# Two-layer convolution kernel: the second channel block convolved by ScalarE and VectorE, statistics on ScalarE, v with two slots

## The chip, the cores and the metric

The kernel runs on one core of a Trainium2 chip. The metric is device time in microseconds, the median of the runs. The core has TensorE (PE) for matrix products, VectorE (DVE), ScalarE (ACT) and GpSimd (POOL) for elementwise work, and SyncE (SP), which issues nearly all DMA transfers. Each engine executes its own instructions in order; semaphores tie the engines together.

## The reference

The input is `x` of shape (16, 56, 56, 384) in fp32. Two layers follow each other:

```
x = x + attention(group_norm(x))     # layer 0
x = x + depthwise(group_norm(x))     # layer 1
```

`group_norm` takes 32 groups of 12 channels, with mean and variance over all 56 x 56 positions of an image. `attention` projects to q, k and v (384 channels each), splits them into three blocks of 128 channels with dilations 1, 2 and 3 and four heads of 32 channels each, and for every position scores q against the nine k at the 3 x 3 neighbours (dilated, zero padded), takes the softmax of the nine, sums the nine v with these weights, and projects back. `depthwise` is a 3 x 3 convolution per channel whose weights are the signs of the given ones, zero padded.

## The kernel before, in words

Channels lie on the partitions in three blocks `j` of 128. An image is cut into seven chunks of eight rows (448 positions), which makes 112 chunks `m`; a chunk is the unit of everything. Three plans give the pieces of work of a chunk. `plan_a` loads `x` and turns it so that channels lie on the partitions (`turn`, L409), takes statistics and writes it to `xd` in device memory. `plan_b` is layer 0: it normalises a chunk of `xd`, projects k and v (`k_or_v`, L467) and q, multiplies q with the shifted k on VectorE (`score`, L508), sums over the head by PE, takes the softmax, spreads the weights over the channels by PE into the PSUM tile `pb_a` (a pool with one buffer), multiplies them with the shifted v on VectorE (`weigh`, L573, L589), adds on GpSimd (L597 to L601), projects back (`out_project`, L607), takes statistics (L621) and writes `x1d`. `plan_c` is layer 1 for one chunk.

The time of a piece is a slice number; a chunk advances by `STEP = 9` slices. Pieces are emitted in the order of (slice, kind), and the framework's scheduler then settles each engine's order, with these as priorities. Layer 1 of a chunk runs ten chunks behind layer 0 of it, since it needs the statistics of the whole image. So in the steady part all three plans run side by side. For the last image, layer 1 runs after everything else.

Layer 1 before the change: channel blocks 0 and 1 (`JG = 2`) are loaded three times with a row's shift as `z` (L694), normalised by four ScalarE instructions (L713), and convolved by PE (`convolve`, L721, twelve products in four column groups, result `pc`), and VectorE adds `x1` (L734). Block 2 is loaded once as `xg`, normalised into the padded tile `zg` (L756), multiplied by nine taps on ScalarE (`taps_g`, L778) and summed on GpSimd (L784 to L792). For the last image block 2 is instead accumulated by VectorE (`taps_last`, L769). Then PE turns the chunk back (`turn`, L794) and ScalarE evacuates it to `osb`, which goes out.

Transposes, projections and convolutions share the PSUM pool `ps_mt` of three buffers. k has two slots per dilation, v has three; each chunk's tile takes border rows from the one before and gives it some, by DMA on SP's queue (L477, L478). Pieces that matter below:

```python
at(t0 - 12 + 3 * g, QKV, lambda g=g: k_or_v(g, 0))
at(t0 - 9 + 3 * g, QKV, lambda g=g: k_or_v(g, 1))
at(t0 + 14 + i, WEIGH, lambda i=i: weigh(i))
at(t0 + 2 + 3 * j + late, CONVOLVE, lambda j=j: convolve(j))
at(t0 + 9 + s, STAGE_C, lambda s=s: turn(s))
```

Of the kernel before, what the change touches and what calls it, by code (L numbers as in the profile page):

```python
# [12 lines left out]
ALU = mybir.AluOpType  # L13
# [15 lines left out]
NPAD = 32  # L29
K_SLOTS, V_SLOTS = 2, 3  # L30
RSQRT_BITS = 0x5F3759DF
# [4 lines left out]
def dilated_attention_then_binary_conv(  # L36
# [36 lines left out]
    K3 = 3 * HD  # L73
    JG = NG - 1

# [61 lines left out]

    ktap = const.tile([P, NTAP], F32, name="ktap")

    kdiag = const.tile([K3, 3, JG * NQ, HD], F32, name="kdiag")  # L140

    xin_p = ctx.enter_context(tc.tile_pool(name="xin_p", bufs=1))
    z_p = ctx.enter_context(tc.tile_pool(name="z_p", bufs=2))
    xa_p = ctx.enter_context(tc.tile_pool(name="xa_p", bufs=3))
    st_p = ctx.enter_context(tc.tile_pool(name="st_p", bufs=2))
# [8 lines left out]
    x1_p = ctx.enter_context(tc.tile_pool(name="x1_p", bufs=2))  # L154
    xg_p = ctx.enter_context(tc.tile_pool(name="xg_p", bufs=2))
    m_p = ctx.enter_context(tc.tile_pool(name="m_p", bufs=2))
    o_p = ctx.enter_context(tc.tile_pool(name="o_p", bufs=2))

# [16 lines left out]


    zg = []
    for s in range(2):
        t = const.tile([P, ROWS + 2, W + 2], F32, name=f"zg_{s}")
        nc.gpsimd.memset(t, 0.0)  # L180
        zg.append(t)
# [12 lines left out]
    def load_small_weights():  # L194

        raw["small"] = t = m_p.tile([P, 3, PX], F32, tag="m", name="small")
        flat = t.rearrange("p k n -> p (k n)")
        at_ = [0]

        def room(parts, n):  # L200
            at_[0] += n
            return flat[:parts, at_[0] - n : at_[0]]

        raw["b"] = room(NG, P)
        raw["k"], raw["kp"] = room(K3, 3 * NG * NQ), room(K3, 3 * NG * NQ)
        raw["kg"] = room(P, NTAP)
        raw["eye"] = room(K3, HD)
        raw["spread"] = room(P, 2 * P)
        raw["clipped"], raw["less"] = room(P, 3 * NG * NQ), room(P, 3 * NG * NQ)
        nc.sync.dma_start(raw["b"], b_proj.rearrange("(j p) -> j p", p=P))  # L210
        nc.sync.dma_start(raw["kg"], w_conv.rearrange("y x c m -> c (y x m)")[JG * P : (JG + 1) * P, :])

# [19 lines left out]
    def small_weights():  # L232
# [29 lines left out]
        kp = raw["kp"].rearrange("p (k s) -> p k s", k=3)  # L262
        binary(ktap, raw["kg"])
        eye3 = raw["eye"]
# [30 lines left out]
    def group_norm(stats, done, for_convolution=False):  # L295
# [79 lines left out]
        return channels, mean, deviation, variance, invert, spread_out  # L375

    def chunk_of(dram, c):
        return dram.rearrange("(j p) n -> p j n", p=P)[:, :, c * PX : (c + 1) * PX]
# [12 lines left out]
    def plan_a(m, t0):  # L391
# [4 lines left out]
        def load():  # L396
            if c == 0:
                stats0[b] = st_p.tile([P, NG, NCH, 6], F32, tag="stats0", name="stats0")
                xd[b] = dr_p.tile([C, H * W], F32, tag="xd", name="xd")
            if b == 0 and c % 3:  # L400

                xin = z_p.tile([P, NQ * PX], F32, tag="z", name="xin_z")[:SUB, : NSUB * C]
                xin = xin.rearrange("p (s c) -> p s c", s=NSUB)
            else:
                xin = xin_p.tile([SUB, NSUB, C], F32, tag="xin", name="xin")
# [3 lines left out]
        def turn(j):  # L409
# [12 lines left out]
            else:  # L422
                xa = xa_p.tile([P, PX], F32, tag="xa", name="xa")
            nc.scalar.copy(xa, pt[:, :PX])  # L424
            nc.vector.bn_stats(stats0[b][:, j, c, :], xa)
            if b:
# [18 lines left out]
    def plan_b(m, t0):  # L445
# [84 lines left out]
        def softmax_1():  # L530

            sT = s_p.tile([P, PX], F32, tag="sT", name="sT")
            nc.scalar.copy(sT, had.pop("ps")[:, :PX])
# [21 lines left out]
        def softmax_3():  # L555

            had["rest"] = rest = s_p.tile([SUB, NSUB * NPAD * HEADS], F32, tag="rest", name="rest")
            nc.scalar.copy(term[0], e8)
# [48 lines left out]
        def out_project(j):  # L607

            if c == 0 and j == 0:
                stats1[b] = st_p.tile([P, NG, NCH, 6], F32, tag="stats1", name="stats1")  # L610
                x1d[b] = dr_p.tile([C, H * W], F32, tag="x1d", name="x1d")
            xr = had["xr"]
            po = ps_mt.tile([P, 512], F32, tag="mt", name="po")
            for g in range(NG):
                nc.tensor.matmul(  # L615
                    po[:, :PX], wprojT[:, g, j * P : (j + 1) * P], had[f"y{g}"], start=(g == 0), stop=(g == NG - 1)
                )
            nc.vector.scalar_tensor_tensor(  # L618
                xr[:, j, :], po[:, :PX], bias[:, j : j + 1], xr[:, j, :], op0=ALU.add, op1=ALU.add
            )  # L620
            nc.vector.bn_stats(stats1[b][:, j, c, :], xr[:, j, :])  # L621
            if j == NG - 1:
# [12 lines left out]
        for g in range(NG):  # L635
            at(t0 - 12 + 3 * g, QKV, lambda g=g: k_or_v(g, 0))
            at(t0 - 9 + 3 * g, QKV, lambda g=g: k_or_v(g, 1))
            at(t0 - 1 + 3 * g, QUERY, lambda g=g: query(g))
# [16 lines left out]
    def plan_c(m, t0):  # L655
# [17 lines left out]
        def load(j):  # L673
# [4 lines left out]
            else:  # L678

                had[f"z{j}"] = []  # L680
                for q0 in range(0, NQ, 2):
                    pool, tag = (t_p, "t") if c % 2 == 0 else (w_p, "w") if (j, q0) != (1, 2) else (xr_p, "xr")
                    z = pool.tile([P, 3, PX], F32, tag=tag, name="z_last")[:K3, :2]
# [33 lines left out]
        def load_x():  # L717
            had["x1"] = x1 = x1_p.tile([P, JG, PX], F32, tag="x1", name="x1")
            nc.sync.dma_start(x1, chunk_of(x1d[b], c)[:, :JG])  # L719

# [18 lines left out]
        def load_g():  # L739
            if b < B - 1:  # L740
                had["xg"] = xg = xg_p.tile([P, ROWS + 2, W], F32, tag="xg", name="xg")
            else:
# [3 lines left out]
                xg[:, lo:hi, :].rearrange("p r w -> p (r w)"),  # L746
                x1d[b][JG * P : (JG + 1) * P, p0 + (lo - 1) * W : p0 + (hi - 1) * W],
            )

        def normalise_g():  # L750
            if c == 0:
                nc.gpsimd.memset(zp[:, 0], 0.0)
            if c == NCH - 1:
# [3 lines left out]
                zp[:, lo:hi, 1 : W + 1], had["xg"][:, lo:hi, :], AF.Identity,  # L757
                bias=mr[:, JG, 0:1], scale=mr[:, JG, 1:2],
            )

        def taps_last(ky):
# [5 lines left out]
            for kx in range(3):  # L767
                o = 3 * ky + kx
                nc.vector.scalar_tensor_tensor(  # L769
                    mid if o == 8 else acc, zp[:, ky : ky + ROWS, kx : kx + W], ktap[:, o : o + 1],  # L770
                    acc if o else mid, op0=ALU.mult, op1=ALU.add,
                )

        def taps_g(ky):
            t = m_p.tile([P, 3, PX], F32, tag="m", name="m")
            for kx in range(3):
                o = 3 * ky + kx
                nc.scalar.activation(  # L778
                    rows(t[:, kx]), zp[:, ky : ky + ROWS, kx : kx + W], AF.Copy, scale=ktap[:, o : o + 1]
                )  # L780
# [13 lines left out]
        def turn(s):  # L794
            pt = ps_mt.tile([P, 512], F32, tag="mt", name="pt_o")
            mid = had["xg"][:, 1 : ROWS + 1, :].rearrange("p r w -> p (r w)")
            for j in range(NG):
                src = mid if j == JG else had["x1"][:, j]
                nc.tensor.transpose(pt[:SUB, j * P : (j + 1) * P], src[:, s * SUB : (s + 1) * SUB], ident)  # L799
            osb = o_p.tile([SUB, C], F32, tag="osb", name="osb")  # L800
            nc.scalar.copy(osb, pt[:SUB, :C])  # L801
# [4 lines left out]
        if b == B - 1:  # L806
# [9 lines left out]
            for ky in range(3):  # L816
                at(t0 + 1 + ky, CONVOLVE, lambda ky=ky: taps_last(ky))
            for s in range(NSUB):
                at(t0 + 12, STAGE_C, lambda s=s: turn(s))
# [10 lines left out]
        for j in range(JG):  # L830
            at(t0 - 4 + 3 * j, LOADS, lambda j=j: load(j))
            at(t0 - 1 + 3 * j + late, NORM, lambda j=j: normalise(j))
            at(t0 + 2 + 3 * j + late, CONVOLVE, lambda j=j: convolve(j))
        for s in range(NSUB):
            at(t0 + 9 + s, STAGE_C, lambda s=s: turn(s))

# [50 lines left out]
```

## Time and profile before

| | |
|---|---|
| median of 3 runs | 5416.96 us (5413.93 to 5419.03) |
| the profiled execution | 5406.89 us |
| its span | 5405.2 us |
| mean granted TensorE clock | 0.98 |
| busy: PE, DVE, ACT, POOL | 5205.9, 4150.0, 2397.8, 4215.2 us |
| DMA | 825.73 MB, mean 153 GB/s |

The profile is of one execution. A row of its groups names the line, the engine, the operation, what it writes and reads with its shape, how often, then busy time, mean duration of one in ns, and the engine's idle time ahead of it with what ended that. A line of waits names who waited for whom, the microseconds in total, the number of waits and the longest. PE's end times are modelled, so a length from start to start says more than the duration printed.

### The profile page before, as it was taken

What the parts mean: (1) busy time and instruction counts of PE and PEld (TensorE: products, weight loads), DVE (VectorE), ACT (ScalarE), POOL (GpSimd) and SP (SyncE); (2) the same over time, 40 slices, a digit from 0 to 9 for tenths busy, and PEclk for the clock granted to TensorE, in tenths of its full rate; (3) what the DMA queues carried; (4) which work ended last, traced back from release to release, by engine and by line L of the source; (5) the groups of instructions that cost most, each with busy time, mean ns of one, the idle gap of its engine ahead of it and who ended that gap; (6) DMA issues with size and microseconds to landing.
All of it is one profiled execution on the core that took longest, in us unless ns stands there. A gap on an engine that the chain in (4) does not pass through costs nothing. (4 is left out here: it accounts for less than half of the span.)

```text
span 5405.2 us, 77297 instructions
## 1 busy us (share of the span) xinstructions
PE 5205.9 (96%) x27669; PEld 2414.4 (45%) x27669; DVE 4150.0 (77%) x4209; ACT 2397.8 (44%) x4189; POOL 4215.2 (78%) x3049
## 2 busy tenths in 40 slices
PE   8999999999999999999999999999999999999965
PEld 4444444444444444444444444444444444444422
DVE  4887777878777787777777777787777778777754
ACT  3224444444444444444444444444444444444433
POOL 2677888888888887888888788888888888888880
PEclk9999999999999999999999999999999999999976
DMA  5444555655555555555655655555555655544443
GB/s 168 127 120 124 159 157 158 163 154 161 158 158 160 164 159 159 157 157 158 163 154 161 164 152 160 164 157 163 159 157 154 164 154 161 161 130 134 122 130 126
DMA packets 810799, 825.73 MB, mean 153 GB/s; under 512 B 359467, under 2 KB 800174, under 8 KB 810414
## 3 DMA queue, kind: packets, MB, share of 16 engines
q1 hardware_dynamic: 802430, 808.79, 54.2%
q10 hardware_dynamic: 7984, 12.00, 0.7%
q8 instruction: 219, 3.59, 0.3%
q14 instruction: 166, 1.36, 0.1%
HBM read 466.41 MB, written 231.21 MB: 129 GB/s over the span
## 5 line engine op out<-in xcount | busy, mean ns | idle before, releaser
L597 POOL TENSOR_TENSOR w<-w 128x1344 f32<-128x1344 f32 x672 | 2049.9, 3050 | 456.2 <-DVE w L589 396.7
L589 DVE TENSOR_TENSOR w<-pb_a,v 128x1344 f32<-128x1344 f32 x1008 | 1559.1, 1547 | 267.0 <-PE pb_a L582 177.4
L516 DVE TENSOR_TENSOR t<-pq,k 128x1344 f32<-128x1344 f32 x1008 | 1535.8, 1549 | 237.0 <-PE pq L463 236.1
L463 PE MATMUL pkv<-xn,wqkvT 128*128 128x448 f32 x3924 | 1569.9, 549 | 9.0 <-ACT xa L424 4.7
L463 PEld LDWEIGHTS pkv<-xn,wqkvT 128*128 128x128 f32 x3924 | 718.4, 190 | 671.8 <-issue 629.4
L615 PE MATMUL po<-y,wprojT 128*128 128x448 f32 x2016 | 834.9, 550 | 27.4 <-POOL y L601 15.0
L784 POOL TENSOR_TENSOR m<-m 128x1344 f32<-128x1344 f32 x210 | 644.7, 3070 | 274.1 <-ACT m L778 274.0
L463 PE MATMUL pq<-xn,wqkvT 128*128 128x448 f32 x1962 | 830.7, 558 | 0.0
L713 ACT ACTIVATE z<-z,mrz 96x448 f32<-96x448 f32 x840 | 578.3, 751 | 350.9 <-DMA z<-x1d 330.3
L501 PE MATMUL ps<-t,sel 128*32 128x448 f32 x6048 | 666.0, 550 | 26.0 <-DVE t L516 25.3
L778 ACT ACTIVATE m<-zg,ktap 128x448 f32<-128x448 f32 x945 | 555.5, 658 | 274.0 <-POOL m L784 266.9
L615 PEld LDWEIGHTS po<-y,wprojT 128*128 128x128 f32 x2016 | 376.4, 191 | 382.9 <-issue 341.1
L727 PE MATMUL pc<-z,kdiag 96*32 96x440 f32 (+1 forms) x5040 | 516.7, 543 | 6.4 <-POOL z L715 4.6
L463 PEld LDWEIGHTS pq<-xn,wqkvT 128*128 128x128 f32 x1962 | 344.0, 189 | 316.9 <-issue 316.9
L734 DVE TENSOR_TENSOR x<-pc,x 128x448 f32<-128x448 f32 x224 | 139.3, 622 | 353.2 <-PE pc L727 342.1
L582 PE MATMUL pb_a<-aT,spread 24*128 24x448 bf16 x3024 | 369.1, 359 | 32.2 <-DVE w L589 25.9
L601 POOL TENSOR_TENSOR y<-y,w 128x448 f32<-128x448 f32 x336 | 381.5, 1135 | 22.6
L618 DVE SCALAR_TENSOR_TENSOR xr<-po,bias,xr 128x448 f32<-128x448 f32 x336 | 227.5, 677 | 220.9 <-PE po L615 217.2
L600 POOL TENSOR_TENSOR y<-w 128x448 f32<-128x448 f32 x336 | 382.2, 1138 | 14.7
L473 ACT COPY v<-pkv 128x448 f32<-128x448 f32 x336 | 178.3, 531 | 484.1 <-PE pkv L463 475.8
L473 ACT COPY k<-pkv 128x448 f32<-128x448 f32 x336 | 178.2, 530 | 376.5 <-PE pkv L463 376.5
L501 PEld LDWEIGHTS ps<-t,sel 128*32 128x32 f32 x6048 | 170.6, 110 | 364.9 <-issue 247.8
(131 smaller groups left out, 4394.7 us busy)
## 6 DMA issues: line engine op xcount, KB each, us to landing
z<-x1d SPq DMA_DIRECT2D x570, 224.0 KB
xr<-xd SPq DMA_DIRECT2D x112, 672.0 KB
x1d<-xr SPq DMA_DIRECT2D x112, 672.0 KB
xn<-xd SPq DMA_DIRECT2D x109, 672.0 KB
xin<-in_x_dram SPq DMA_DIRECT2D x108, 672.0 KB
xd<-xa SPq DMA_DIRECT2D x315, 224.0 KB
out_dram<-osb SPq DMA_DIRECT2D x420, 168.0 KB
x<-x1d SPq DMA_DIRECT2D x112, 448.0 KB
```

The lines of the kernel that those rows point to most:

```text
L463: nc.tensor.matmul(dst[:, :PX], wqkvT[:, cc, o0 : o0 + P], had["xn"][:, cc, :], start=(cc == 0), stop=(cc == NG - 1))
L501: return nc.tensor.matmul(had["ps"][32 * j : 32 * j + 32, :PX], sel[:, s0 : s0 + 32], tk, start=(issued[j] == 1), stop=(issued[j] == len(r ...
L516: nc.vector.tensor_tensor(t.rearrange("p k (r w) -> p k r w", w=W), q3, k3, ALU.mult)
L589: nc.vector.tensor_tensor(w.rearrange("p k (r w) -> p k r w", w=W), pb[:, :, :PX].rearrange("p k (r w) -> p k r w", w=W), three(kv[1][g][m ...
L597: nc.gpsimd.tensor_tensor(w0, w0, w, ALU.add)
L600: nc.gpsimd.tensor_tensor(y, w0[:, 0], w0[:, 1], ALU.add)
L601: nc.gpsimd.tensor_tensor(y, y, w0[:, 2], ALU.add)
L615: nc.tensor.matmul(po[:, :PX], wprojT[:, g, j * P : (j + 1) * P], had[f"y{g}"], start=(g == 0), stop=(g == NG - 1))
L713: nc.scalar.activation(z, z, AF.Identity, bias=mrz[:, j, q, 0:1], scale=mrz[:, j, q, 1:2])
L727: return nc.tensor.matmul(pcr[q * HD : (q + 1) * HD, :, lo:hi], kdiag[:, kx, j * NQ + q, :], rows(set_of(j, q))[:, :, lo + kx - 1 : hi + k ...
L778: nc.scalar.activation(rows(t[:, kx]), zp[:, ky : ky + ROWS, kx : kx + W], AF.Copy, scale=ktap[:, o : o + 1])
L784: nc.gpsimd.tensor_tensor(had["m"], had["m"], t, ALU.add)
```

## The change

Layer 1 keeps PE for block 0 alone (`JG = 1`). Block 2 (`JS = 2`) stays as it was. Block 1 is convolved in a new way: `load_b` loads it once as `xb`, `normalise_b` normalises it into a third padded tile, `taps_b` multiplies it by the nine taps on ScalarE into nine slices of the tile `m9`, `load_summand` loads the block itself into a tenth slice, and `sum_b` sums the ten on VectorE in four parts of 112 positions. `m9` and `xb` have one buffer each. The `BATCH_NORM_STATS2` instructions on VectorE go: the sum of a tile comes from an accumulator output of the instruction that writes it, ScalarE scales it to the mean and sums the squared deviations by a second accumulator output (`statistics`). v of a chunk is computed nine slices later and has two slots. Pools shrink to make room (`z_p` 2 to 1, `xa_p` 3 to 2), and `rest` shares its buffer with `sT`. The diff, without the declarations of pools and the loading of the small weights, which follow from it:

```diff
-K_SLOTS, V_SLOTS = 2, 3
+K_SLOTS, V_SLOTS = 2, 2
-    JG = NG - 1
+    JG = 1
+    JS = NG - 1
+    NB = NG - JG
...
-    z_p = ctx.enter_context(tc.tile_pool(name="z_p", bufs=2))
-    xa_p = ctx.enter_context(tc.tile_pool(name="xa_p", bufs=3))
+    z_p = ctx.enter_context(tc.tile_pool(name="z_p", bufs=1))
+    xa_p = ctx.enter_context(tc.tile_pool(name="xa_p", bufs=2))
...
+    m9_p = ctx.enter_context(tc.tile_pool(name="m9_p", bufs=1))
+    xb_p = ctx.enter_context(tc.tile_pool(name="xb_p", bufs=1))
...
+    def new_statistics(name):
+        stats = st_p.tile([P, NG, NCH, 3], F32, tag=name, name=name)
+        nc.gpsimd.memset(stats[:, :, :, 0:1], float(PX))
+        return stats
+
+    def statistics(entry, xa, total):
+        nc.scalar.mul(entry[:, 1:2], total, 1.0 / PX)
+        squares = st_p.tile([P, PX], BF16, tag="squares", name="squares", bufs=1)
+        nc.scalar.activation(
+            squares, xa, AF.Square, bias=entry[:, 1:2], scale=-1.0, accum_out=entry[:, 2:3]
+        )
...
-            if b == 0 and c % 3:
+            if b == 0 and c % 2:
...
-            nc.scalar.copy(xa, pt[:, :PX])
-            nc.vector.bn_stats(stats0[b][:, j, c, :], xa)
+            total = st_p.tile([P, 1], F32, tag="total", name="total")
+            nc.scalar.activation(xa, pt[:, :PX], AF.Copy, accum_out=total)
+            statistics(stats0[b][:, j, c, :], xa, total)
...
             nc.vector.scalar_tensor_tensor(
-                xr[:, j, :], po[:, :PX], bias[:, j : j + 1], xr[:, j, :], op0=ALU.add, op1=ALU.add
-            )
-            nc.vector.bn_stats(stats1[b][:, j, c, :], xr[:, j, :])
+                xr[:, j, :], po[:, :PX], bias[:, j : j + 1], xr[:, j, :], op0=ALU.add, op1=ALU.add, accum_out=total
+            )
+            statistics(stats1[b][:, j, c, :], xr[:, j, :], total)
...
-            at(t0 - 9 + 3 * g, QKV, lambda g=g: k_or_v(g, 1))
+            at(t0 + 3 * g, QKV, lambda g=g: k_or_v(g, 1))
...
-            nc.sync.dma_start(x1, chunk_of(x1d[b], c)[:, :JG])
+            nc.sync.dma_start(x1[:, :JG], chunk_of(x1d[b], c)[:, :JG])
...
+        def load_b():
+            had["xb"] = xb = xb_p.tile([P, ROWS + 2, W], F32, tag="xb", name="xb")
+            nc.sync.dma_start(
+                xb[:, lo:hi, :].rearrange("p r w -> p (r w)"),
+                x1d[b][JG * P : (JG + 1) * P, p0 + (lo - 1) * W : p0 + (hi - 1) * W],
+            )
+
+        zb = zg[2]
+
+        def normalise_b():
...
+            nc.scalar.activation(
+                zb[:, lo:hi, 1 : W + 1], had["xb"][:, lo:hi, :], AF.Identity,
+                bias=mr[:, JG, 0:1], scale=mr[:, JG, 1:2],
+            )
+
+        def load_summand():
+            had["m9"] = m9 = m9_p.tile([P, NTAP + 1, PX], F32, tag="m9", name="m9")
+            nc.sync.dma_start(m9[:, NTAP], x1d[b][JG * P : (JG + 1) * P, p0 : p0 + PX])
+
+        def taps_b(o):
+            ky, kx = divmod(o, 3)
+            nc.scalar.activation(
+                rows(had["m9"][:, o]), zb[:, ky : ky + ROWS, kx : kx + W], AF.Copy, scale=ktap[:, 0, o : o + 1]
+            )
+
+        def sum_b(s):
+            part = slice(s * SUB, (s + 1) * SUB)
+            nc.vector.reduce_sum(
+                had["x1"][:, JG, part], had["m9"][:, :, part].rearrange("p o n -> p n o"), axis=AX.X
+            )
...
+            at(t0 - 4, LOADS, load_b)
+            at(t0 + 2, NORM, normalise_b)
+            at(t0 + 2, LOADS, load_summand)
+            for o in range(NTAP):
+                at(t0 + 3 + o // 3, CONVOLVE, lambda o=o: taps_b(o))
+            for s in range(NSUB):
+                at(t0 + 7 + s, CONVOLVE, lambda s=s: sum_b(s))
...
+        at(t0 - 1, LOADS, load_b)
+        at(t0 + 1, NORM, normalise_b)
+        at(t0 + 1, LOADS, load_summand)
+        for o in range(NTAP):
+            at(t0 + 2 + (0, 1, 1, 1, 2, 3, 3, 3, 4)[o], CONVOLVE, lambda o=o: taps_b(o))
         for s in range(NSUB):
+            at(t0 + 7 + s, CONVOLVE, lambda s=s: sum_b(s))
             at(t0 + 9 + s, STAGE_C, lambda s=s: turn(s))
```

The first group of times in the last two blocks is that of the last image.

## The prediction

> **What bounds the kernel now.** I read the page's busy shares, then whole-image stretches of the steady part, then who keeps TensorE (PE) waiting, one stretch in order of time, and the rows of the operations concerned. The page first:
>
> ```profile
> PE 5205.9 (96%) x27669; PEld 2414.4 (45%) x27669; DVE 4150.0 (77%) x4209; ACT 2397.8 (44%) x4189; POOL 4215.2 (78%) x3049
> ```
>
> A stretch of seven chunks, one image (columns: window, length, busy time of PE, weight loads, VectorE, ScalarE, GpSimd; clock, DMA share, GB/s):
>
> ```profile
> 1251.00:1574.00 323.00, 319.78 (x1729) 149.23 (x1729) 257.44 (x259) 151.88 (x266) 267.63 (x186) 1.00 0.58 160
> ```
>
> So a chunk takes 323/7 = 46.1 us, PE idles 0.5 of it, VectorE (DVE) is busy 36.8, ScalarE (ACT) 21.7, GpSimd 38.2. PE sets the pace. The view of PE's waits says for what little it stands still:
>
> ```profile
> PE pb_a L582 <- DVE w L589: 25.9, 25, 4.7
> PE ps L501 <- DVE t L516: 25.3, 34, 1.7
> ```
>
> First in it stands the broadcast of the weights `pb_a`, whose PSUM buffer is single: each needs VectorE's product `w` of the one before. PE's work in order of time (start, length, operation) gives what each piece takes of PE, from start to next start:
>
> ```profile
> 3023.73 0.38 PE L799 MATMUL pt_o<-ident,x 128*112 128x128 f32 x2
> 3023.95 0.27 PE L799 MATMUL pt_o<-ident,xg 128*112 128x128 f32 x1
> 3024.15 0.36 PE L582 MATMUL pb_a<-aT,spread 24*128 24x448 bf16 x3
> 3024.45 0.35 PE L331 MATMUL pv<-dev,gsel 128*32 128x1 f32 x6
> 3024.73 0.60 PE L412 MATMUL pt_x<-ident,xin 112*128 112x112 f32 x4
> 3025.26 1.71 PE L501 MATMUL ps<-t,sel 128*32 128x448 f32 x16
> 3026.79 2.41 PE L727 MATMUL pc<-z,kdiag 96*32 96x448 f32 x24
> 3029.13 0.36 PE L582 MATMUL pb_a<-aT,spread 24*128 24x448 bf16 x3
> ```
>
> One convolution holds PE for 3029.13 - 3026.79 = 2.34 us; an input transpose 0.53, a score burst 1.53, an output transpose 0.42, a broadcast 0.30. Two k/v projections took 4.62 (3019.11 to 3023.73), a query projection 2.45 (3014.68 to 3017.13).
>
> The rows that price the rest (busy, mean ns of one):
>
> ```profile
> L516 DVE TENSOR_TENSOR t<-pq,k 128x1344 f32<-128x1344 f32 x1008 | 1535.8, 1549 | 237.0 <-PE pq L463 236.1
> L734 DVE TENSOR_TENSOR x<-pc,x 128x448 f32<-128x448 f32 x224 | 139.3, 622 | 353.2 <-PE pc L727 342.1
> L541 DVE TENSOR_REDUCE mx<-pt_s 112x48 f32<-112x432 f32 x112 | 66.8, 596 | 1.7 <-PE pt_s L536 1.7
> L547 DVE TENSOR_REDUCE sm<-ew 112x48 f32<-112x432 f32 x112 | 101.1, 903 | 0.0
> L778 ACT ACTIVATE m<-zg,ktap 128x448 f32<-128x448 f32 x945 | 555.5, 658 | 274.0 <-POOL m L784 266.9
> L713 ACT ACTIVATE z<-z,mrz 96x448 f32<-96x448 f32 x840 | 578.3, 751 | 350.9 <-DMA z<-x1d 330.3
> ```
>
> [...]`mx` and `sm` reduce the same 432 elements at a stride of 12 elements, `mx` from PSUM in 596 ns, `sm` from SBUF in 903. [...]
>
> **The part that decides: `sum_b`.** It reduces ten slices, 1120 elements, for 112 results, at a stride of 448 elements in SBUF. From 1344 and 448 elements (1549 and 622 ns) VectorE's contiguous rate is 1.035 ns an element and 149 to 158 ns fixed. Lower bound: 1120 x 1.035 + 149 = 1.31 us. At `sm`'s rate, (903 - 149)/432 = 1.745 ns: 1120 x 1.745 + 149 = 2.10 us. The real stride is longer than `sm`'s; if its excess over the contiguous rate were half as large again, 2.09 ns, it is 2.49 us; nothing bounds it above. I take 2.10: like `sm`[...]. Start to start it is 0.05 less, as two `t` take 3.01 us in the timeline where the row says 2 x 1.55.
>
> **The change part by part, steady chunk.**
>
> PE loses one convolution: -2.34 us.
>
> VectorE: six BATCH_NORM_STATS2 (208.1 + 191.0 us busy over 651, 0.61 each) go, -3.7; one add of `pc` goes, -0.6; four sums come, 4 x 2.05 = +8.2; the accumulator output of `xr`, three times[...], I take nothing, since its row idles 220.9 us for PE. Sum +3.9, to 40.7 of the 43.8 us that PE would leave. It still fits on average, so what matters is where the sums stand. In the built order of the changed kernel three of seven chunks (the others are like them) have on VectorE, from the broadcast after which the sums begin: w, t, t, sum, w, sum, sum, w, and then PE's next broadcast but two may start. PE's work between the same two broadcasts is: broadcast, two k/v projections, output transpose (0.30 + 4.62 + 0.42); broadcast, input transpose, score burst, a third of a query projection (0.30 + 0.53 + 1.53 + 0.82); broadcast, two thirds of a query and of a k/v projection (0.30 + 1.63 + 1.54): 12.0 us. VectorE's chain is five products of 1.5 = 7.5, three sums, and 0.5 for the two hand-overs (w starts 0.1 to 0.3 after the broadcast's 0.36): 8.0 + 3 x sum. It closes without a stall up to a sum of 1.33 start to start; at 2.05 it is 14.15, and PE stands 2.15 us. The chunks with another order (sum, t, t, add, w, t, sum, sum, w, sum) come to about the same by the same working. Behind the waiting broadcast stands everything on PE. Hence -2.34 + 2.15 = -0.2 us per chunk.
>
> ScalarE: nine taps at 0.59 (555.5/945) = +5.3; `zb` +0.84; four `z` go, -2.75; six squares at the 0.69 that `z` costs, +4.1; [...]. From 21.7 to about 31 of 46 us. That is covered as long as PE's three `mt` buffers are emptied in time; the multiply for `stats1` waits for VectorE's `xr` with evacuations queued behind it, which PE waits for. Without cover each microsecond is PE's. I set 0.1 us per chunk and cancel it against PE's present 0.5 of idleness, part of which lies in the same waits.
>
> DMA on SP's queue: three `z` transfers (672 KB) and half of `x1` (224) go, `xb` (280) and the summand (224) come: fewer bytes at a DMA share of 0.58. The summand's issue waits for the fourth sum with the next loads behind it; those are planned three to nine slices of 5 us ahead of use, so nothing. `v` nine slices later keeps its place in the chunk's rhythm; its borders now have five slices, 25 us, instead of fourteen before the products need them; nothing. `z_p` and `xa_p` with fewer buffers serve fewer tiles: nothing, else a wait of ACT for `z` of the kind that now totals 330.3 us off PE's path.
>
> Head: the statistics of the first image move from VectorE to ScalarE, [...]in a stretch in which ACT was busy 16.7 of the first 50 us; some shows: +6. Tail: seven chunks of the last image took 5405 - 5268 = 137 us, waiting for `z_last` transfers. Half of these go; VectorE then needs per chunk 9 x 0.68 (`taps_last`) + 8.2 + 0.62 + 0.51 = 15.5, that is 108 plus some 14 for filling: -15.
>
> **Sum.** 105 steady chunks x -0.2 = -21; head +6; tail -15: -30 on the span of 5405.2, that is 5375; the profiled execution took 5406.9, the median of the runs is 5417.0. On the median: 5387.
>
> **Rivals.** A, sum near the contiguous rate (1.3 us): no stall, 105 x -2.34 = -246, tail 22 us better still, +6, and up to 30 for ACT: -250 to -280, some 5150. For it: nothing bounds the stride's price but one row. Against: that row's shortest of 112 is 889 ns. B, sum dearer than `sm`'s rate: at 2.49, PE stands 3 x (2.44 - 1.33) = 3.3, +1.0 per chunk, +105, tail -4, head +6: 5525; it decides from 2.1 us start to start, where the stall equals the convolution. For it: the stride is 37 times that of `sm`. C, ScalarE's queue: if evacuations behind `total`'s wait hold PE 1 us per chunk, +105 on my forecast, 5490; against it, ACT has a third of its time free. D, that the tensor work doesn't go away, is excluded: the built order has twelve convolution products per chunk instead of 24.
>
> **How the numbers follow.** My case 0.45, own range 5340 to 5440 (0.1 us in the sum is 0.3 x 105 = 32 us); A, with everything down to 1.7 us, 0.22; B 0.23; C 0.10. The range, 5165 to 5530, leaves out the outer ends of A and B. A measurement of this kernel tells 0.2%, 11 us. My case is faster in 0.65 of itself, the same in 0.15, slower in 0.2. Faster 0.22 + 0.29 = 0.51, same 0.07, slower 0.33 + 0.09 = 0.42.
>
> **What would show it.** The row of the sums at about 2.1 us, x448; `pb_a` waiting for `w` at the head of PE's waits with about 200 us instead of 25.9; PE's busy time near 4945 us; VectorE near 88%; ACT near 64%. Wrong if the sum is far from 2.1, or if PE's new idle time is put down to ACT or a DMA.

## The result, and the profile after

The changed kernel takes 5602.79 us (median of four runs, 5593.23 to 5607.71) where the kernel before takes 5417.40 on the same chip: a ratio of 1.0341, with an interval of 1.0323 to 1.0359. It is slower by 185 us; the forecast was 30 us faster, and its range ended at 5530.

The page of the changed kernel, its line of busy times (span 5606.0 us, mean granted TensorE clock 0.957 instead of 0.980):

```profile
PE 5099.4 (91%) x24597; PEld 2373.3 (42%) x24597; DVE 4633.9 (83%) x4202; ACT 3320.1 (59%) x7220; POOL 4214.9 (75%) x3040
```

The matrix products fell by 3072 (2688 of the convolution, 384 tiny ones of the statistics), and yet PE's busy time fell by only 106 us, not by the 112 x 2.34 = 262 that these products had taken. So the products that stayed became longer. Next, rows of the groups (busy, mean ns of one, idle time before and what ended it), the first of the kernel before, the others of the changed one:

```profile
L463 PE MATMUL pkv<-xn,wqkvT 128*128 128x448 f32 x3924 | 1569.9, 549 | 9.0 <-ACT xa L424 4.7 <-ACT osb L801 2.8
L486 PE MATMUL pkv<-xn,wqkvT 128*128 128x448 f32 x3924 | 1697.7, 581 | 91.3 <-ACT xa L447 51.2 <-DVE xr L642 35.6 <-ACT osb L865 3.2
L831 DVE TENSOR_REDUCE x<-m 128x112 f32<-128x1120 f32 x448 | 937.5, 2116 | 104.9 <-ACT m L825 76.8 <-ACT xn L482 16.7 <-DMA m<-x1d 5.3
```

The sums of ten take 2116 ns, where the forecast had 2100. The projections of k and v have the same 3924 products in both kernels; one takes 581 ns instead of 549. The head of PE's waits (us in total, number, longest):

```profile
PE pb_a L605 <- DVE w L612: 214.6, 162, 3.4
PE pkv L486 <- ACT xa L447: 51.2, 27, 3.2
PE pt_o L860 <- DVE x L831: 37.6, 21, 5.0
PE pkv L486 <- DVE xr L642: 35.6, 17, 3.0
```

The broadcast `pb_a` waits for VectorE's product `w` for 214.6 us; the forecast had said about 200 in place of 25.9. Here is one such wait in order of time (start, length, engine, operation, idle time before it in brackets):

```profile
2331.51 3.01 DVE L539 TENSOR_TENSOR t<-pq,k 128x1344 f32<-128x1344 f32 x2
...
2334.51 2.17 DVE L831 TENSOR_REDUCE x<-m 128x112 f32<-128x1120 f32 x1
...
2336.59 1.55 DVE L612 TENSOR_TENSOR w<-pb_a,v 128x1344 f32<-128x1344 f32 x1
...
2338.06 4.14 DVE L831 TENSOR_REDUCE x<-m 128x112 f32<-128x1120 f32 x2
...
2342.12 1.54 DVE L612 TENSOR_TENSOR w<-pb_a,v 128x1344 f32<-128x1344 f32 x1
...
2343.72 0.37 PE L605 MATMUL pb_a<-aT,spread 24*128 24x448 bf16 x3 [1.95 <-DVE w L612]
```

VectorE has no gap between 2331.51 and 2343.66; PE, which finished its own work at 2341.77, stands until the last `w` is done. With the 0.20 us at the broadcast before, that is 2.15 us in this chunk, the very stall of the forecast's chain. So the chain that the forecast was built on is there at its size, and the loss comes on top of it.

Two things come on top. The first is seen on PE alone, in what follows two stalls of the same length:

```profile
2343.72 0.37 PE L605 MATMUL pb_a<-aT,spread 24*128 24x448 bf16 x3 [1.95 <-DVE w L612]
2344.01 4.97 PE L486 MATMUL pkv<-xn,wqkvT 128*128 128x448 f32 x8
2348.82 2.42 PE L638 MATMUL po<-y,wprojT 128*128 128x448 f32 x6
...
2390.59 0.37 PE L605 MATMUL pb_a<-aT,spread 24*128 24x448 bf16 x3 [1.97 <-DVE w L612]
2390.89 3.27 PE L486 MATMUL pkv<-xn,wqkvT 128*128 128x448 f32 x8
2394.00 2.42 PE L638 MATMUL po<-y,wprojT 128*128 128x448 f32 x6
```

The same eight products take 4.81 us from start to start behind the first stall and 3.11 behind the second, one chunk later. The view by windows of 6 us behind each (length, busy time of PE, weight loads, VectorE, ScalarE, GpSimd; then clock, DMA share, GB/s) names the difference:

```profile
2343.70:2349.70 6.00, 5.98 (x14) 2.84 (x14) 6.00 (x5) 3.52 (x7) 3.26 (x4) 0.72 0.59 160
2390.60:2396.60 6.00, 6.00 (x20) 2.76 (x19) 6.00 (x5) 2.93 (x6) 3.23 (x4) 1.00 0.45 131
```

After the first stall the granted clock has a mean of 0.72, after the second 1.00. The clock records have a period of half speed from 2345.0 to 2348.4, 3.4 us; half of that, 1.70 us, is what the products lost.

The clock records also tell the two stalls apart. From 100 us on, all 85 half-clock periods of the changed kernel start on a grid of 3.413 us, within 0.005 us. The first stall lies within one stretch of this grid, 2341.58 to 2344.99: PE idles 1.95 us of it, and the next stretch is at half clock. The second is split by the grid at 2389.36 into 0.74 and 1.23 us, and no half clock follows. Over all stretches at full clock between 500 and 4900 us, half clock follows none of the 1126 in which PE idles less than 1.5 us, 4 of the 24 with 1.5 to 1.85 us, and 63 of the 64 with more.

Between 500 and 4900 us of the span the records show 17.1 us at half speed before and 256.2 after. The same stretch in the view by windows, kernel before:

```profile
500.00:4900.00 4400.00, 4345.71 (x23405) 2023.33 (x23404) 3474.62 (x3482) 2062.00 (x3605) 3608.16 (x2507) 1.00 0.58 158
```

and the changed kernel:

```profile
500.00:4900.00 4400.00, 4092.13 (x19938) 1909.12 (x19937) 3719.78 (x3338) 2707.43 (x5895) 3452.67 (x2400) 0.97 0.52 144
```

The second thing is the border between two images. There ScalarE's queue reads, in order of time:

```profile
2514.51 2.34 ACT L825 ACTIVATE m<-zg,ktap 128x448 f32<-128x448 f32 x4
2516.89 0.85 ACT L813 ACTIVATE zg<-xb,mr 128x560 f32<-128x560 f32 x1
2517.64 0.52 ACT L447 ACTIVATE xa<-pt_x 128x448 f32<-128x448 f32 x1
```

Four taps and a normalisation, without a gap, stand ahead of the evacuation `xa` of an input transpose. On PE, at that time:

```profile
2518.31 1.90 PE L486 MATMUL pkv<-xn,wqkvT 128*128 128x448 f32 x3 [2.83 <-ACT xa L447]
```

The projection wants the PSUM buffer that `xa` empties, and stands 2.83 us. How this falls on the chunks of an image is seen when chunks are measured on PE, from the first product of one chunk's output projection (`po`) to that of the next, and averaged over ten images, the fourth to the thirteenth, by their place. In this table the time at half clock is from the clock records; the last two columns are two experiments told below, `e1_sum_contig` and `e7_pairs_bn`.

| place | before, us | after, us | at half clock, after | e1 | e7 |
|---|---|---|---|---|---|
| 0 | 48.2 | 53.5 | 5.5 | 49.6 | 47.8 |
| 1 | 47.1 | 46.8 | 1.7 | 45.6 | 47.3 |
| 2 | 48.0 | 53.0 | 4.8 | 49.4 | 46.7 |
| 3 | 44.9 | 46.4 | 1.7 | 44.0 | 42.9 |
| 4 | 44.9 | 46.6 | 1.7 | 44.1 | 43.1 |
| 5 | 44.9 | 47.1 | 2.7 | 44.5 | 46.4 |
| 6 | 46.4 | 44.6 | 0 | 45.6 | 45.0 |
| image | 324.4 | 337.9 | 18.1 | 322.7 | 319.2 |

An image takes 13.6 us more, 1.94 per chunk; 105 x 1.94 = 204 us. The head, up to the first store of `x1d`, is 3.5 us longer (179.7 to 176.2), the tail behind the last one 8.9 shorter (149.6 to 158.5). That makes 199 of the 200.8 us between the two spans. Places 0 and 2 carry 10.3 of the 13.6. In the ordinary chunks, 3 to 5, the kernel lost 5.4 us together, and 6.1/2 = 3.1 of lost clock is in that. With the clock set aside they are still 0.8 us each slower, where the forecast had them 0.2 faster: PE idles 2.6 us in each, 2.17 of it at `pb_a` and 0.4 at `pt_x`, where it idled none before, and its products take only 1.8 us less. The convolution's own fall by 2.23, from 4.46; the others take 0.5 more.

### The profile page after: what moved, and what is told of

Same layout as the page of the kernel before. It is cut to its first block, busy times and chain, and to the rows that moved or that the text cites. A ratio compares the mean times of both kernels' runs of the same rounds, so it can differ in the third digit from the quotient of the medians.

```text
span 5606.0 us, 74316 instructions
## 1 busy us (share of the span) xinstructions
PE 5099.4 (91%) x24597; PEld 2373.3 (42%) x24597; DVE 4633.9 (83%) x4202; ACT 3320.1 (59%) x7220; POOL 4214.9 (75%) x3040
## 5 line engine op out<-in xcount | busy, mean ns | idle before, releaser
L486 PE MATMUL pkv<-xn,wqkvT 128*128 128x448 f32 x3924 | 1697.7, 581 | 91.3 <-ACT xa L447 51.2
L486 PEld LDWEIGHTS pkv<-xn,wqkvT 128*128 128x128 f32 x3924 | 762.1, 202 | 822.3 <-issue 703.2
L831 DVE TENSOR_REDUCE x<-m 128x112 f32<-128x1120 f32 x448 | 937.5, 2116 | 104.9 <-ACT m L825 76.8
L486 PE MATMUL pq<-xn,wqkvT 128*128 128x448 f32 x1962 | 857.1, 566 | 0.0
L839 ACT ACTIVATE m<-zg,ktap 128x448 f32<-128x448 f32 x945 | 570.7, 658 | 298.4 <-POOL m L845 296.1
L825 ACT ACTIVATE m<-zg,ktap 128x448 f32<-128x448 f32 x1008 | 607.0, 657 | 202.2 <-DVE x L831 198.0
L524 PE MATMUL ps<-t,sel 128*32 128x448 f32 x6048 | 662.2, 547 | 13.9 <-DVE t L539 13.5
L605 PE MATMUL pb_a<-aT,spread 24*128 24x448 bf16 x3024 | 372.1, 361 | 220.1 <-DVE w L612 214.6
L605 PEld LDWEIGHTS <-spread 24*128 24x128 bf16 x3024 | 113.1, 91 | 704.0 <-issue 676.6
L737 ACT ACTIVATE z<-z,mrz 96x448 f32<-96x448 f32 x420 | 290.1, 749 | 113.3 <-DMA z<-x1d 79.8
```

Of the source, the lines that this page charges most:

```text
L486: nc.tensor.matmul(dst[:, :PX], wqkvT[:, cc, o0 : o0 + P], had["xn"][:, cc, :], start=(cc == 0), stop=(cc == NG - 1))
L524: return nc.tensor.matmul(had["ps"][32 * j : 32 * j + 32, :PX], sel[:, s0 : s0 + 32], tk, start=(issued[j] == 1), stop=(issued[j] == len(r ...
L605: return nc.tensor.matmul(pb[:, kx, :PX].rearrange("p (s n) -> p s n", s=NSUB), spread[rows_of, v % 2, :], had["a"][rows_of, :, v // 8, :] ...
L825: nc.scalar.activation(rows(had["m9"][:, o]), zb[:, ky : ky + ROWS, kx : kx + W], AF.Copy, scale=ktap[:, 0, o : o + 1])
L831: nc.vector.reduce_sum(had["x1"][:, JG, part], had["m9"][:, :, part].rearrange("p o n -> p n o"), axis=AX.X)
L839: nc.scalar.activation(rows(t[:, kx]), zp[:, ky : ky + ROWS, kx : kx + W], AF.Copy, scale=ktap[:, JS - JG, o : o + 1])
```

## The experiments

Two theories were on the table. The first: the stride of the sums decides, by the stalls of `pb_a` and by the half clock that these start. The second: ScalarE's new work, the statistics above all, holds PE. Ratios are to the kernel before, run beside each.

### e1_sum_contig: sums of the same length without the stride

```diff
-                had["x1"][:, JG, part], had["m9"][:, :, part].rearrange("p o n -> p n o"), axis=AX.X
+                had["x1"][:, JG, part], had["m9"].rearrange("p o n -> p (o n)").rearrange("p (n q o) -> p n q o", q=NSUB, o=NTAP + 1)[:, :, s, :], axis=AX.X
```

The order of the instructions is that of the changed kernel on every engine; only the addresses from which the sum reads differ.

> The changed kernel with each of the four sums reading ten neighbouring elements for a result instead of ten at a stride of 448; same number of instructions, same order on every engine. Leaves out: the second block's sums are of the wrong elements. Theory 1 (the stride's price stalls TensorE, and the stalls bring its clock to half for some microseconds each): the sum's row falls from 2.12 to 1.3 to 1.4 us, PE's wait of pb_a for w from 214.6 to under 40 us, the granted clock rises from 0.957 to 0.975 or more, time 5160 to 5260. Theory 2 (ScalarE's longer queue empties the projections' buffers late, and that sets the pace at the image boundary): the same fall of the row, but the waits of pkv for ACT and DVE stay near 90 us, and the time stays above 5400.

Measured: 5375.36 us, 0.9928 (0.9913 to 0.9943). Its row of the sums:

```profile
L831 DVE TENSOR_REDUCE x<-m 128x112 f32<-128x1120 f32 x448 | 575.6, 1308 | 148.9 <-ACT m L825 78.7 <-ACT xn L482 33.4 <-DMA m<-x1d 27.8
```

and its waits of PE:

```profile
PE pkv L486 <- ACT xa L447: 61.8, 29, 2.8
PE pb_a L605 <- DVE w L612: 44.2, 32, 4.2
PE pt_x L434 <- PE pkv L486: 41.3, 50, 0.9
```

The sum takes 1308 ns, the forecast's lower bound (1.31 us) to the nanosecond; `pb_a` waits 44.2 us instead of 214.6, and the half clock between 500 and 4900 us falls from 256.2 to 91.9. With one view changed, more than the whole loss is gone. So the stride of the sums decides the sign. As PE has the same products to do in both, the two pages also say how the loss divides: from e1 to the changed kernel the span grows by 233.2 us, PE's idle time (span less busy) by 147.6, from 359.0 to 506.6, and its busy time by 85.6; half of what the clock records have more at half speed over the whole run, (484.6 - 301.1)/2, is 91.8. Products that are the same got longer by the lost clock: of what the stride costs, some five eighths are stalls and three eighths clock. But 5375 is not the 5150 of rival A, and it lies between the two theories' expectations. The chunks in places 3 to 5 are 0.7 us shorter each, not 2.34: PE idles 1.1 us in each, 0.9 of it in `pt_x` for `pkv` (the third wait above; the profile doesn't tell what lies behind it), and its products fall by 1.7 us, not by the convolution's 2.23. Places 0 and 2 take 2.7 us more together than before the change, with 6.1 us at half clock. There the first wait above stands, `pkv` for `xa`, which the edit doesn't shorten.

### e2_sum_half: two of the four sums with the stride, two without

```diff
-                had["x1"][:, JG, part], had["m9"][:, :, part].rearrange("p o n -> p n o"), axis=AX.X
+                had["x1"][:, JG, part], (had["m9"].rearrange("p o n -> p (o n)").rearrange("p (n q o) -> p n q o", q=NSUB, o=NTAP + 1)[:, :, s, :] if s % 2 == 0 else had["m9"][:, :, part].rearrange("p o n -> p n o")), axis=AX.X
```

> As the run before with two of the four sums made contiguous, the other two as in the changed kernel; same order. Leaves out: half of the second block's sums are of the wrong elements. A dose between: by the chain of the forecast (two cheap sums and one dear one between the broadcasts) PE would stand 8.0 + 1.3 + 1.3 + 2.05 - 12.0 = 0.65 us per chunk instead of 2.15. Theory 1: pb_a waits for w 50 to 90 us in total; if half clock comes only behind long stalls it is nearly gone and the time is 5230 to 5320; if half clock follows any idle time in proportion, the clock is half way, 0.966, and the time 5350 to 5420. Theory 2: above 5450.

Measured: 5441.32 us, 1.0048 (1.0033 to 1.0063). One stall of an ordinary chunk, PE in order of time:

```profile
2279.58 0.37 PE L605 MATMUL pb_a<-aT,spread 24*128 24x448 bf16 x3 [0.54 <-DVE w L612]
2279.88 3.27 PE L486 MATMUL pkv<-xn,wqkvT 128*128 128x448 f32 x8
```

The chain of the forecast, with two of its three sums at 1.25 from start to start and one at 2.05, gives 8.0 + 2.50 + 2.05 - 12.0 = 0.55 us; measured 0.54. (The expectation had 0.65, with 1.3 for each cheap sum.) No half clock follows: the eight products take 3.11 us. In places 3 to 5 of the image, where e1 has neither stalls of `pb_a` nor half clock, the three chunks take 134.3 us against 132.6: 1.6 = 3 x 0.54, the stall one for one. In the changed kernel the three have 6.5 us of such stalls and 6.1 us at half clock, and take 140.1, 7.5 more than e1; waits of `pt_x` for `pkv`, 2.6 us in e1 and 1.2 here, go the other way, and the rest isn't assigned. Half of the stride thus costs 66 us (e1 to e2) and the second half about 160. Most of that bend is in the chain itself, which has slack for a first part of the price: 0.55 us of stall for the first half, 1.6 for the second. The clock bends the same way: over the whole run PE's idle time grows by 48.1 us and its busy time by 22.1 in the first step (half of the added half-clock time: 20.3), by 99.5 and 63.5 in the second (71.4). The clock was not varied by itself: no run fills the stalls with idle products, which would change the order of the other work too.

### e3_interleaved and e6_pairs: other layouts for the ten

In e3 the ten summands of a result lie side by side, and the taps write at a stride of ten; the tenth is copied by ScalarE from `xb`:

```diff
-            had["m9"] = m9 = m9_p.tile([P, NTAP + 1, PX], F32, tag="m9", name="m9")
-            nc.sync.dma_start(m9[:, NTAP], x1d[b][JG * P : (JG + 1) * P, p0 : p0 + PX])
+            had["m9"] = m9 = m9_p.tile([P, PX, NTAP + 1], F32, tag="m9", name="m9")
+            nc.scalar.copy(rows(m9[:, :, NTAP]), had["xb"][:, 1 : ROWS + 1, :])
...
-                rows(had["m9"][:, o]), zb[:, ky : ky + ROWS, kx : kx + W], AF.Copy, scale=ktap[:, 0, o : o + 1]
+                rows(had["m9"][:, :, o]), zb[:, ky : ky + ROWS, kx : kx + W], AF.Copy, scale=ktap[:, 0, o : o + 1]
...
-                had["x1"][:, JG, part], had["m9"][:, :, part].rearrange("p o n -> p n o"), axis=AX.X
+                had["x1"][:, JG, part], had["m9"][:, part, :], axis=AX.X
...
-            at(t0 + 2, LOADS, load_summand)
+            at(t0 + 2, CONVOLVE, load_summand)
```

> The changed kernel with m9 laid out position by position: ten neighbouring elements for one result, so that the sums read contiguously and are right; the taps are written at a stride of ten elements, and the tenth comes by a ScalarE copy from xb instead of a DMA. Theory 1: sums 1.3 to 1.4 us, time 5180 to 5280 if ScalarE writes the stride at its present 0.66 us per tap; up to 5400 if the taps double, 1.2 us. Theory 2: ScalarE's added copy and dearer taps make it slower than 5600.

Measured: 5641.45 us, 1.0414 (1.0398 to 1.0430). Its rows of the taps and of the sums:

```profile
L825 ACT ACTIVATE m<-zg,ktap 128x448 f32<-128x448 f32 x1008 | 945.3, 1078 | 2.7 <-ACT osb_last L865 2.0 <-DMA z_last<-x1d 0.7
...
L831 DVE TENSOR_REDUCE x<-m 128x112 f32<-128x1120 f32 x448 | 576.8, 1308 | 241.2 <-ACT m L825 162.6 <-PE pt_o L860 76.6 <-ACT v L496 1.9
```

and the head of PE's waits:

```profile
PE pkv L486 <- ACT xa L447: 93.2, 29, 3.9
PE pt_o L860 <- ACT v L496: 87.1, 55, 2.7
```

The sum is cheap, but the stride has moved to ScalarE's writes: a tap takes 1078 ns instead of 657, nine of them 3.8 us more per chunk. VectorE now waits for the taps and PE for ScalarE's evacuations, and the half clock comes back (276.5 us) with no `pb_a` stall at the head. The second theory's expectation, slower than 5600, came true. It is the mechanism of rival C, by the taps instead of the statistics: an engine busy for two thirds of the time decides, by what is queued behind its long stretches.

In e6 two summands lie side by side, five such pairs for a result; `load_summand` is moved as in e3:

```diff
-            had["m9"] = m9 = m9_p.tile([P, NTAP + 1, PX], F32, tag="m9", name="m9")
-            nc.sync.dma_start(m9[:, NTAP], x1d[b][JG * P : (JG + 1) * P, p0 : p0 + PX])
+            had["m9"] = m9 = m9_p.tile([P, (NTAP + 1) // 2, PX, 2], F32, tag="m9", name="m9")
+            nc.scalar.copy(rows(m9[:, NTAP // 2, :, NTAP % 2]), had["xb"][:, 1 : ROWS + 1, :])
...
-                rows(had["m9"][:, o]), zb[:, ky : ky + ROWS, kx : kx + W], AF.Copy, scale=ktap[:, 0, o : o + 1]
+                rows(had["m9"][:, o // 2, :, o % 2]), zb[:, ky : ky + ROWS, kx : kx + W], AF.Copy, scale=ktap[:, 0, o : o + 1]
...
-                had["x1"][:, JG, part], had["m9"][:, :, part].rearrange("p o n -> p n o"), axis=AX.X
+                had["x1"][:, JG, part], had["m9"][:, :, part, :].rearrange("p a n i -> p n a i"), axis=AX.XY
```

> The changed kernel with m9 in five pairs of slices, the two of a pair side by side for each position, so that a sum reads two neighbours, then steps; taps written at a stride of two elements; the tenth by a ScalarE copy from xb instead of a DMA. The sums are right. [...]the sum's row 1.3 to 1.45 us, taps 0.66 to 0.8 us, time 5370 to 5430. If every step away from dense order pays: the row 1.7 to 2.1 us, time 5450 to 5600.

Measured: 5378.78 us, 0.9944 (0.9928 to 0.9961). Its rows of the taps and of the sums:

```profile
L825 ACT ACTIVATE m<-zg,ktap 128x448 f32<-128x448 f32 x1008 | 633.2, 702 | 4.0 <-ACT osb_last L865 2.0 <-DMA z_last<-x1d 2.0
L831 DVE TENSOR_REDUCE x<-m 128x112 f32<-128x1120 f32 x448 | 576.8, 1308 | 139.0 <-ACT m L825 93.0 <-PE pt_o L860 46.0
```

Pairs give the sum the rate of ten in a row, 1308 ns as in e1, although the pairs of one result are 448 x 2 elements apart; and the taps pay only 45 ns for writing every second element. All three figures, 1308 ns, 702 ns and the time, lie in the first ranges of the expectation, those for the case that two neighbours are enough. This run computes the right sums, and its time agrees with e1's.

### e4_before_stats, e8_before_v: two parts of the change alone, on the kernel before

e4 takes `new_statistics`, `statistics`, their calls and the shared buffer of `rest` into the kernel before:

```diff
-            nc.scalar.copy(xa, pt[:, :PX])
-            nc.vector.bn_stats(stats0[b][:, j, c, :], xa)
+            total = st_p.tile([P, 1], F32, tag="total", name="total")
+            nc.scalar.activation(xa, pt[:, :PX], AF.Copy, accum_out=total)
+            statistics(stats0[b][:, j, c, :], xa, total)
```

> The kernel before with the statistics alone moved to ScalarE as in the change. Theory 1: ScalarE gains 6 to 7 us of work per chunk and VectorE loses 3.7, both off the path; 5390 to 5430, no change beyond 0.3%. Theory 2: waits of PE for ScalarE's evacuations of xa, k and v rise by 50 us or more, and the time is 5460 or more.

Measured: 5432.73 us, 1.0035 (1.0025 to 1.0045). Its waits of PE, the two at the head:

```profile
PE pb_a L596 <- DVE w L603: 24.2, 13, 5.9
PE pkv L477 <- ACT xa L438: 24.2, 14, 1.9
```

`pkv` for `xa` is 24.2 us instead of 4.7, the other head line is nearly unchanged (25.9 before). The waits stand in place 2 of the image, which takes 52.1 us instead of 48.0 and has 4.1 us at half clock on average instead of 0.3. So the statistics on ScalarE cost some 20 us on the kernel before, at the image's border: 0.35%, just above the first theory's expectation, and not the loss.

e8 takes only the places of `v`:

```diff
-K_SLOTS, V_SLOTS = 2, 3
+K_SLOTS, V_SLOTS = 2, 2
...
-            at(t0 - 9 + 3 * g, QKV, lambda g=g: k_or_v(g, 1))
+            at(t0 + 3 * g, QKV, lambda g=g: k_or_v(g, 1))
```

> The kernel before with v alone computed nine slices later and two slots. Forecast: no change, 5400 to 5430, the borders' DMA in time. If the borders come late: DVE waits for DMA of v, PE behind it at pb_a, 5450 or more.

Measured: 5398.49 us, 0.9981 (0.9973 to 0.9989). A gain of 0.2%, where nothing was forecast; not a cost, in any case.

### e5_contig_bn, e7_pairs_bn, e9_after_bn: the statistics back on VectorE

The same edit on e1, on e6 and on the changed kernel:

```diff
-            total = st_p.tile([P, 1], F32, tag="total", name="total")
-            nc.scalar.activation(xa, pt[:, :PX], AF.Copy, accum_out=total)
-            statistics(stats0[b][:, j, c, :], xa, total)
+            nc.scalar.copy(xa, pt[:, :PX])
+            nc.vector.bn_stats(stats0[b][:, j, c, :], xa)
...
-            statistics(stats1[b][:, j, c, :], xr[:, j, :], total)
+            nc.vector.bn_stats(stats1[b][:, j, c, :], xr[:, j, :])
```

> The contiguous sums of the first experiment, and the statistics back on VectorE as before the change. Leaves out: the second block's sums are of the wrong elements. Theory 1b (what is left above the forecast's lower case, some 200 us, is ScalarE's statistics: its queue empties xa, k and v late, 62 us of waits of pkv for ACT xa and 41 of pt_x, and half clock behind them): these waits fall below 30 us together, time 5200 to 5290. Rival (VectorE is the tighter engine even with cheap sums, and 3.7 us more per chunk put it in the way): pb_a waits for w rise from 44 to over 100 us, time 5380 or more.

Measured: 5387.11 us, 0.9959 (0.9944 to 0.9974); 0.3% more than e1, by the two ratios. The time is the rival's; `pb_a` waits 74.3 us, between the two expectations.

> The pairs with the statistics back on VectorE. If both things hold, cheap pairs and ScalarE's statistics as the rest: 5200 to 5320, faster than both kernels. If VectorE gets in the way: 5380 or more.

Measured: 5321.80 us, 0.9837 (0.9822 to 0.9852); 57 us less than e6. Its waits of PE at the head:

```profile
PE pb_a L602 <- DVE w L609: 94.7, 94, 2.8
PE ps L521 <- DVE t L536: 44.1, 60, 1.7
```

> The changed kernel with the statistics alone put back on VectorE; the dear sums stay. If the chain of sums on VectorE sets the pace, the 3.7 us of statistics per chunk on the same engine make it worse: pb_a waits for w 300 us or more, 5650 to 5900. If ScalarE's queue set the pace, it becomes better than 5560.

Measured: 5604.99 us, 1.0357 (1.0340 to 1.0375); the same as the changed kernel (1.0341), within the intervals; neither expectation came true. Its first two waits of PE:

```profile
PE pb_a L602 <- DVE w L609: 179.8, 179, 3.1
PE ps L521 <- DVE t L536: 54.7, 69, 1.7
```

In all three PE waits less for `xa` and more for VectorE. In e6 these had been, in PE's waits:

```profile
PE pkv L486 <- ACT xa L447: 62.9, 29, 2.9
PE pb_a L605 <- DVE w L612: 23.4, 18, 5.7
```

In e7 the wait for `xa` is gone, and places 0 and 2 of the image take 94.5 us, less than before the change (96.2), with 1.7 us at half clock, where e6 has 9.2. The price is on VectorE: `pb_a` goes from 23.4 to 94.7 us. In e9, where the strided sums fill VectorE, the exchange is even: PE's waits for `xa` fall from 51.2 to 19.5 us, all those for VectorE together rise from 325.1 to 353.9, and the border stays slow (103.5 us in places 0 and 2, with 9.2 at half clock). In e5 48.7 us of the wait for `xa` stay, and the edit gains nothing. So these runs give no single answer to whether ScalarE or VectorE should have the statistics; it seems to depend on what else their queues hold at the border. The second theory's waits are real, but the statistics moved the time by 0.35% in e4 and by 1.1% from e6 to e7, and by nothing or the other way in e9 and e5: they are not what makes the change slower. e7 beats both kernels: it is 87 us under the kernel before, measured beside it on the same chip (5409.17), and by the ratios 5% under the changed one.

### e10_pairs_two_sums: fewer and longer sums

```diff
-            part = slice(s * SUB, (s + 1) * SUB)
+            part = slice(2 * s * SUB, 2 * (s + 1) * SUB)
```

with two sums per chunk in place of four, in e7.

> The pairs with statistics on VectorE, and two sums of 224 results in place of four of 112: by the contiguous rate 2240 x 1.035 + 0.15 = 2.47 us each, 0.3 us less VectorE per chunk. If VectorE's total work is what still holds PE: 10 to 30 us better than with four, 5290 to 5315. If its longest uninterrupted piece is: PE stands behind each, pb_a waits for w above 95 us, 5330 to 5400.

Measured: 5469.41 us, 1.0108 (1.0092 to 1.0125). Its row of the sums:

```profile
L827 DVE TENSOR_REDUCE x<-m 128x224 f32<-128x2240 f32 x224 | 553.1, 2472 | 55.6 <-ACT m L821 55.5
```

and its first three waits of PE:

```profile
PE pb_a L602 <- DVE w L609: 66.2, 73, 3.5
PE pv L340 <- POOL dev L334: 43.5, 14, 3.4
PE pt_s L556 <- ACT sT L553: 40.8, 27, 2.8
```

VectorE does less (553.1 us of sums instead of 577), `pb_a` waits less than in e7, and the kernel is slower by 2.7 points of the ratio, with 143.3 us at half clock between 500 and 4900 us in place of 51.2. The due times put other work around the fewer sums, and other waits came up. The time is above both expectations. The run changes two things at once and says nothing on its question; it does show that less busy time on VectorE did not make the kernel faster.

## Why the prediction was wrong

- **What bounds the kernel, the removal of the convolution:** right. In an ordinary chunk the convolution's products hold PE 2.23 us instead of 4.46, against the forecast's 2.34.
- **The price of `sum_b`:** right, 2116 ns for 2.10 us, and the lower bound too (1308 ns). The rate of `sm`, 1.75 ns an element at a stride of 12, holds at a stride of 448 (1.76); that it would was the author's estimate, and why it does is not shown. Rival B falls.
- **The chain of VectorE between two broadcasts:** right, 2.15 us in an ordinary chunk, and its threshold as well (0.54 for 0.55 in e2). That the other orders come to about the same: 2.92, 2.09 and 2.17 us for `pb_a` in places 0 to 2 and none in place 6, a mean of 1.95 per chunk.
- **"Hence -2.34 + 2.15 = -0.2 us per chunk": wrong, for want of a term.** A stall was priced at its length. In the changed kernel's stretch from 500 to 4900 us PE has 118 stalls of more than 1 us, and 65 of them have a half-clock period of at least 3.4 us close behind; before, there were 12, all under 1.5 us, and five such periods. A period of 3.4 us cost 1.70 (4.81 less 3.11 for the eight products above). Per chunk that is 0.09 us of lost clock before and 1.41 after: +1.32, on 105 chunks 139 us. It explains PE's busy time as well: 5099 instead of 4945, and 135 of these 154 us are half of the 271 us by which the half-clock time of the whole run grew. The trace of the kernel before already holds the term in its five periods, each 3.41 us long. The clock records of both kernels have two values, 1.0 and 0.5, and of the 85 periods of the changed kernel 69 last 3.41 us. A stretch of the grid need not be idle throughout: with 1.85 us of idle PE or more in it, half clock followed 63 times of 64. The stall of 1.95 us shown above lies within one stretch and half clock followed it, the grid splits the one of 1.97 us and none did; of all stalls between 1.5 and 2.0 us, 33 of 62 were followed by it.
- **"I set 0.1 us per chunk and cancel it against PE's present 0.5 of idleness": wrong in size.** PE's idle time per chunk, from the two lines of windows, went from 0.57 to 3.38 us: +2.81. `pb_a` for `w` is 1.86 of it; the other 0.95 is mostly waits for `xa` and `xr`, some for `k` and `v`, at the image's border. For the waits on ScalarE, rival C had named the mechanism, at 1 us per chunk, and got 0.10 of the chances; in the wait shown above it is the taps that stand ahead, not the wait for `total`. The argument against it, that ScalarE has a third of its time free, was an average; at the border it has 3.2 us of taps and normalisation ahead of the evacuation.
- **The sum with both terms:** -2.34 + 2.81 + 1.32 = +1.79 us per chunk, against +1.94 measured. The other 0.15 is in PE's products: at full clock they fall by about 2.2 us per chunk (45.68 to 43.50, from the two lines of windows with the lost clock taken off), not by 2.34.
- **Head and tail:** +3.5 for +6 and -8.9 for -15; signs right, both about half as large. **ScalarE** is busy 59% for 64; its additional work was sized well. About 2 of the forecast's 31 us per chunk, for the small multiplies and the accumulator outputs, were the author's estimate, and the +6 of the head rests partly on the same; in the rows of the changed kernel they take 2.9 us per chunk (134.3 us of multiplies at 200 ns, 192.7 of accumulator reads at 187 to 197). **VectorE** 83% for 88. DMA cost little (PE's waits for it go from 21 to 31 us in total), and `v` nothing, as forecast; alone it even gained 0.2%.
- **Rival A**: with the sum at its price, in e1, the stalls of `pb_a` are gone in places 2 to 6, but its time is some 225 us too low, since it too left out PE's other waits and the clock. In e1 PE idles 13.5 us per image, 4.0 before, and has 6.1 us at half clock, 1.7 before. How that divides between taps, statistics, the smaller pools and the order of the queues is open; the pools were not varied by themselves, and e6 and e7 show only that the statistics are a part.

## What to carry to other kernels

Here PE was the bound, and a new wait of 1.95 us cost 1.70 us on top of its length. So look for half-clock periods behind the stalls that are already there, and for how much idle time within the grid's stretches they follow: here 1.85 us or more in a stretch of 3.41 us was followed by one 63 times of 64, while stalls of 0.54 us cost their length alone (e2). Price a strided reduction from a strided row that the kernel already has, and before accepting the price try two partners of the sum side by side: here pairs took the sum from 2116 to 1308 ns, for 45 ns on each writer. And test the free time of an engine where its longest uninterrupted stretch lies, at the border of two images, not as a share of the span.

## What the runs showed of the hardware that was not expected

- In the changed kernel stalls of PE between 1.5 and 2.0 us were followed by a half-clock period in 33 of 62 cases, those between 2.5 and 3.0 us in 19 of 27. Of its 85 periods from 100 us on, 69 last 3.41 us and 9 twice that, and they start on a grid of 3.413 us. In all twelve traces together, between 500 and 4900 us, a stretch at full clock was followed by half clock in 219 of 222 cases with 1.9 us or more of idle PE in it, and in 23 of 14625 with less than 1.5.
- The price of a strided fp32 reduction on VectorE was the same at strides of 48 and 1792 bytes, (2116 - 149)/1120 = 1.76 ns an element in the changed kernel against 1.75 for `sm` in the kernel before, and it vanished when the elements lay in adjacent pairs (1308 ns in e6, as for ten in a row in e1).
- ScalarE paid for strided writes as well: 448 results took 657 ns dense (the changed kernel), 702 at every second element (e6), 1078 at every tenth (e3).
- In the changed kernel each ScalarE instruction with an accumulator output comes with a second one, `ACTIVATION_READ_ACCUMULATOR`, of 187 to 197 ns; on VectorE the 336 of `xr` come with a `DVE_READ_ACCUMULATOR` of 83 ns. The kernel before has no row of either, so what the forecast took for them was the author's estimate.
